# Gating of expert blocks in two steps, and a denser order of the last state-space scan, in a Perceiver layer

## The chip, the cores and the metric

The kernel runs on one core of a Trainium2 chip. The metric is the device time of one execution in microseconds (us). A profile is one execution taken by the hardware profiler; its times count from the start of its span.

## What is computed

`x` is 4 batches of 256 tokens of width 256, `ctx` 4 batches of 4096 context rows. Three residual layers follow each other, each on a layernorm of `x`:

```
x = x + xattn(layernorm(x), ctx)     # 8 heads of 64; keys and values from ctx and from x itself
x = x + mixed(layernorm(x))          # router: the top 64 tokens of a batch -> attention, the other 192 -> state-space model
x = x + moe(layernorm(x))            # 8 experts of hidden width 512, the best 2 of each token

# state-space core of `mixed` (per batch, 192 tokens, 512 channels, 16 states)
xi, z = split(u @ in_w); xc = silu(conv4(xi)); delta = softplus(dtp @ dt_w + dt_b)
h_t = exp(delta * A) * h_{t-1} + delta * xc * B_t;   y_t = sum over states of C_t * h_t
y = (y + xc * Dp) * silu(z) @ out_w

# one expert
y = (silu(x @ w_gate.T) * (x @ w_up.T)) @ w_down.T
```

The router ranks the 256 scores of a batch (how many are greater, ties by index), and a permutation built from the ranks puts the chosen tokens behind the others.

## The kernel before, in words

All is float32. The cross attention fills the first 1270 us or so: 16 groups (a batch and a pair of heads), each in 8 steps, with the order of every engine's work written out by hand. Beside it run "generators" for the other two layers: pieces of work that end in `yield due, cost`. A clock in the program (`now`) is moved on by hand-given lengths of the main work; at each call of `slot(budget)` (line 1168) every generator that is due and whose VectorE cost fits into what is left of the budget gets one step. So the numbers behind `yield` decide where on each engine's queue a piece stands. Each engine then works its queue in order and waits on semaphores.

Once the cross attention is done, batch 3 has still to go through `mixed` while the routed experts of the first six token tiles (batches 0 to 2) are at work. This is the stretch that the change touches:

- `ordered` (line 1687) works through 19 blocks of 128 gathered tokens. Block j has a gate half (`half(j, 0)`, tile p0b, 16 matmul passes) and an up half (p1b) into PSUM tiles of one tag with three buffers, then `turn_block(j + 1)` (transposes of the next block's rows into psxb, on TensorE, then a copy xTb on ScalarE), then the down half of block j - 1 (pdb, line 1746, from its gated tile hb), then the gating of block j. Weights are loaded three blocks ahead through SP's queue, rows gathered through GpSimd's.
- `gated` (line 1675) is tanh on ScalarE (line 1678), (tanh + 1) * gate on VectorE (line 1679, tile sg, which frees the gate half's PSUM buffer) and the product with the up half on VectorE (line 1683, tile hb, which frees the up half's).
- `router` (line 232) for batch 3: layernorm on ScalarE, transposes psxn, hidden psh, scores pssc, then the ranks on VectorE in two halves of 128 tokens (lines 288 to 296), `top` (line 300), positions psn, permutation `perm`, gathered tokens psg.
- `ssm_front`/`front_late` (line 603): four psin products with a convolution on VectorE each, then pspr, then psdt and the softplus (Abs, Exp, Ln on ScalarE, lines 669 to 675), then eight small products.
- `ssm_scan_late` (line 777): 16 steps (4 state groups by 4 channel tiles). A step is four exponentials on ScalarE (`decay`, one step ahead, three buffers), and on VectorE a product (line 838), the scan itself (839), a product (845) and an addition (846) into a tile `db` of a tag with four buffers; `sums` (line 810) then adds it into PSUM with two matmuls by the identity, one step behind. B and C come by broadcasting loads on ScalarE's queue (line 795), two state groups ahead.
- `ssm_back` (line 857): gate, out_w product (pssd), back to token order (psback), residual; then `prepare` (line 1810): layernorm, transposes (psx, line 1824), router logits (pslg) for the dense experts. `experts` (line 1852) runs all 8 experts on batch 3's two tiles, pg and pu (line 1868) and pde (line 1881); it needs `prepare`.

Of the kernel before, what the change touches and what calls it, by code (L numbers as in the profile page):

```python
# [8 lines left out]
F32 = mybir.dt.float32  # L9
AF = mybir.ActivationFunctionType  # L10
ALU = mybir.AluOpType
# [3 lines left out]
P = 128  # L15
# [9 lines left out]
NBOT = T - KTOP  # L25
DIN, DS, DC, DTR = 512, 16, 4, 16
NDT = DIN // P
# [19 lines left out]
def perceiver_layer(ctx: ExitStack, tc: tile.TileContext, a: dict, out: bass.AP):  # L47
    nc = tc.nc
# [183 lines left out]
    def router(b, st):  # L232
# [21 lines left out]
        for c in range(KD):  # L254
# [7 lines left out]
            out=lower, in_=lower, compare_op=ALU.is_gt, fill=0.0, base=0,  # L262
# [3 lines left out]
        hs = bg.tile([P, 2, T], F32, tag="r3", name="hT_srow")  # L266
# [21 lines left out]
        for h in range(2):  # L288
            eq = bg.tile([P, T], F32, tag="r4", name="eq")
            for other, op0, op1 in (  # L290
                (lower[:, h, :], ALU.is_equal, ALU.mult), (eq, ALU.is_gt, ALU.add),
            ):
                nc.vector.scalar_tensor_tensor(
                    out=eq, in0=srow, scalar=scol[:, h : h + 1], in1=other, op0=op0, op1=op1
                )
            nc.vector.tensor_reduce(out=rank[:, h : h + 1], in_=eq, axis=AX.X, op=ALU.add)
            if h == 0 and not late:
                yield 0.5, 1.6
        top = small.tile([P, 2], F32, name="top")
        nc.vector.tensor_scalar(  # L300
            out=top, in0=rank, scalar1=float(KTOP), scalar2=None, op0=ALU.is_lt
        )
        yield (4.5 if late else 1.0), 1.4

        ps = bank("psn")
        nc.tensor.matmul(ps[:, 0:1], cs["tri"], top[:, 0:1], start=True, stop=True)
# [296 lines left out]
    def front_late(b, st, ws, conv):  # L603

        ua, xc, zs, delta = st["ua"], st["xc"], st["zs"], st["delta"]
        pool = late["pool"]
        th = pool.tile([P, NDT, NBOT], F32, tag="ul", name="th")
        pss = {}  # L610

        def silu(m):
            nc.vector.scalar_tensor_tensor(
                out=xc[:, m, :], in0=th[:, m, :], scalar=1.0, in1=xc[:, m, :],
                op0=ALU.add, op1=ALU.mult,
            )

        st["dt_w"] = pool.tile([DTR, DIN], F32, name="dt_wl")
        nc.scalar.dma_start(out=st["dt_w"], in_=a["dt_w"])
        yield 0.9, 0  # L620
        for m in range(NDT + 2):
            if m < NDT:
                ps = pss[m] = bank("psin")
                for j in range(2):
                    for c in range(KD):
                        nc.tensor.matmul(
                            ps[:, j * NBOT : (j + 1) * NBOT], ws[m][:, j, c, :],
                            ua[:, c, :NBOT], start=(c == 0), stop=(c == KD - 1),
                        )
                nc.scalar.activation(  # L630
                    xc[:, m, :], ps[:, :NBOT], AF.Identity, bias=cs["conv_b"][:, m : m + 1],
                    scale=cs["conv_w"][:, m, DC - 1 :],
                )
                nc.scalar.activation(zs[:, m, :], ps[:, NBOT : 2 * NBOT], AF.Copy, scale=0.5)
            if 1 <= m <= NDT:
                conv(m - 1, pss[m - 1])
                nc.scalar.activation(th[:, m - 1, :], xc[:, m - 1, :], AF.Tanh)
            if m >= 2:
                silu(m - 2)
            yield 0.9, 0  # L640
        projT = bg.tile([DTR + 2 * DS, NBOT], F32, tag="projT", name="projT")
        ps = bank("pspr")
        for m in range(NDT):
            nc.tensor.matmul(
                ps[: DTR + 2 * DS, :NBOT], cs["xproj"][:, m, :], xc[:, m, :],
                start=(m == 0), stop=(m == NDT - 1),
            )
        nc.scalar.copy(projT, ps[: DTR + 2 * DS, :NBOT])

        bcd = st["bcd"] = dram.tile([2, DS, NBOT], F32, tag="bcd", name="bcd")  # L650
        nc.scalar.dma_start(
            out=bcd.rearrange("o s t -> (o s) t"), in_=projT[DTR:, :]
        )
        st["late"] = ssm_scan_late(b, st)
        yield 0.9, 0

        ev = bg.tile([P, NDT, NBOT], F32, tag="y", name="ev")
        for i in range(2):
            ps = bank("psdt")
            for j in range(2):  # L660
                m = 2 * i + j
                nc.tensor.matmul(
                    ps[:, j * NBOT : (j + 1) * NBOT], st["dt_w"][:, m * P : (m + 1) * P],
                    projT[:DTR, :], start=True, stop=True,
                )
            for j in range(2):
                m = 2 * i + j
                v = ps[:, j * NBOT : (j + 1) * NBOT]
                nc.scalar.activation(ev[:, m, :], v, AF.Abs, bias=cs["dt_b"][:, m : m + 1])
                nc.vector.tensor_scalar(  # L670
                    out=delta[:, m, :], in0=v, scalar1=cs["dt_b"][:, m : m + 1], scalar2=0.0,
                    op0=ALU.add, op1=ALU.max,
                )
        nc.scalar.activation(ev, ev, AF.Exp, scale=-1.0)
        nc.scalar.activation(ev, ev, AF.Ln, bias=1.0)
        next(st["late"])
        yield 5.4, 0
        u = st["u"] = pool.tile([P, NDT, NBOT], F32, tag="ul", name="ul")
        for m in range(NDT):
            nc.vector.tensor_tensor(delta[:, m, :], delta[:, m, :], ev[:, m, :], ALU.add)  # L680
            nc.vector.tensor_tensor(u[:, m, :], xc[:, m, :], delta[:, m, :], ALU.mult)
            if m == 0:
                next(st["late"])
        st["scanning"] = True
# [92 lines left out]
    def ssm_scan_late(b, st):  # L777
# [3 lines left out]
        SG = 4  # L781
        K = DS // SG
# [27 lines left out]
        def sums(i):  # L810
            k, m = divmod(i, NDT)
            for s in range(SG // 2):
                nc.tensor.matmul(
                    yps[:, m // 2, (m % 2) * NBOT : (m % 2 + 1) * NBOT], ident, dbl[i][:, s, :],
                    start=False, stop=(k == K - 1 and m % 2 == 1 and s == SG // 2 - 1),
                )

        dbl = {}
# [1 line left out]
        load(1)  # L820

        yps = st["yps"] = late["psum"].tile([P, 2, 512], F32, name="yps")
        zero = pool.tile([P, SG, NBOT], F32, tag="dbl", name="zero", bufs=4)[:, :2]
        nc.gpsimd.memset(zero, 0.0)
        for i in range(2):
            nc.tensor.matmul(
# [7 lines left out]
        for i in range(K * NDT):  # L834
            k, m = divmod(i, NDT)
            decay(i + 1)
            db = dbl[i] = pool.tile([P, SG, NBOT], F32, tag="dbl", name="db", bufs=4)
            nc.vector.tensor_tensor(db, spread[k, 0], bc(u[:, m, :], 1, SG), ALU.mult)
            nc.vector.tensor_tensor_scan(
                out=db.rearrange("p s t -> p (s t)"),  # L840
                data0=das[i % 3].rearrange("p s t -> p (s t)"),
                data1=db.rearrange("p s t -> p (s t)"),
                initial=0.0, op0=ALU.mult, op1=ALU.add,
            )
            nc.vector.tensor_tensor(db, db, spread[k, 1], ALU.mult)
            nc.vector.tensor_tensor(db[:, : SG // 2], db[:, : SG // 2], db[:, SG // 2 :], ALU.add)
            if i:
                sums(i - 1)
            if m == NDT - 1:
                load(k + 2)  # L850
            if i == 5:
                start(gate_late(b, st))
            yield 3.9, 3.8
        sums(K * NDT - 1)
        yield 1.5, 0

# [791 lines left out]
    with ExitStack() as s4, tc.manual_schedule():  # L1648
# [23 lines left out]
        def load_expert(e):  # L1672
            return [load_part(e, i) for i in range(3)]

        def gated(pg, pu, out, n):

            sg = fk.tile([P, 512], F32, name="sg")
            nc.scalar.activation(sg[:, :n], pg[:, :n], AF.Tanh, scale=0.5)
            nc.vector.scalar_tensor_tensor(
                out=sg[:, :n], in0=sg[:, :n], scalar=1.0, in1=pg[:, :n],  # L1680
                op0=ALU.add, op1=ALU.mult,
            )
            nc.vector.tensor_tensor(out, sg[:, :n], pu[:, :n], ALU.mult)

        first = {}

        def ordered():
# [72 lines left out]
            for j in range(4):  # L1760
                gather(j)
            turn_block(0)
            for j in range(NB):
                pg = yield from half(j, 0)
                load(j + 3, 0)
                pu = yield from half(j, 1)
                load(j + 3, 1)
                turn_block(j + 1)
                gather(j + 4)
                rest = down(j - 1)  # L1770
                yield next(rest, 0.9)

                hs[j] = fk.tile([P, NHC, P], F32, name="hb")
                gated(pg, pu, hs[j].rearrange("p m i -> p (m i)"), 512)
                yield from rest
                if j:
                    load(j + 2, 2)
# [115 lines left out]
        while "ready" not in order:  # L1893
            now[0] += 1.0
            slot(5.0)
        late["prepare"] = prepare
        now[0] += 1.0
        slot(5.0)
        for took in ordered():
            now[0] += took  # L1900
            slot(5.0)
        while "x4T" not in dense:
# [50 lines left out]
```

## Time and profile before

| | us |
|---|---|
| median of the runs (lowest, highest) | 1538.34 (1537.46, 1538.44) |
| the profiled execution's own time | 1534.16 |
| its span | 1532.4 |
| busy: TensorE matmul, VectorE, ScalarE, GpSimd | 1452.4, 1062.5, 758.1, 411.9 |
| end of the last cross attention matmuls (po, line 1449) | 1272.3 |
| first scan step of batch 3 (line 838) | 1327.5 |
| end of the last scan step (line 846) | 1422.2 |
| first dense expert matmul (pg, line 1868) | 1441.9 |

A row of the trace gives the start, the length, the engine, the line, the operation, the tiles written and read, their sizes and how many instructions are merged into it; in square brackets stands the idle time of the engine before it and what ended that. The granted clock is the share of TensorE's full clock that it was allowed. A float32 matmul shows as two passes, so one psum group of 4 by 2 matmuls is a row of 16. Ends of matmuls are modelled, and rows that follow each other overlap a little.

### The profile page before, as it was taken

To read this page: it belongs to the slowest core of one execution; us is meant where nothing else is said; L and a number is where in the kernel's file an instruction comes from. 1 tells how busy PE (TensorE), PEld (TensorE's weight loads), DVE (VectorE), ACT (ScalarE), POOL (GpSimd) and SP (SyncE) were. 2 spreads that over 40 slices of the span, in tenths; PEclk is the share of its full clock that TensorE was granted. 3 is DMA by queue.
4 is the path that set the end of the run, shared out by engine and by line. 5 is a ranking of instruction groups with operands and counts; after the bars stand their busy time and mean duration, and the time that the engine had idled before them with its cause. 6 is when DMAs were issued, how large, how long until landed. Compare 5 with 4: busy or idle time off the path is not lost.

```text
span 1532.4 us, 37303 instructions
## 1 busy us (share of the span) xinstructions
PE 1452.4 (95%) x15686; PEld 1034.5 (68%) x15686; DVE 1062.5 (69%) x1825; ACT 758.1 (49%) x1484; POOL 411.9 (27%) x465
## 2 busy tenths in 40 slices
PE   7999999999999999999999999999998968899899
PEld 3657676677666566675756665757574757888687
DVE  1666665656589986565899956666999663689453
ACT  3444454455566645454766544656655523544211
POOL 1000000000069960000499800001999101210110
PEclk9999999999999999999999999999999979999999
DMA  6455434424345443424445444352643333788461
GB/s 229 142 158 152 157 116 150 154 85 131 109 145 179 138 131 121 148 82 144 144 135 174 135 134 130 103 163 73 182 157 99 105 131 109 244 272 283 136 203 49
DMA packets 157767, 223.41 MB, mean 146 GB/s; under 512 B 14976, under 2 KB 76160, under 8 KB 157600
## 3 DMA queue, kind: packets, MB, share of 16 engines
q1 hardware_dynamic: 149632, 208.96, 43.3%
q10 hardware_dynamic: 6480, 8.00, 1.6%
q0 software_dynamic: 1488, 4.07, 1.0%
q8 instruction: 124, 2.03, 0.5%
q14 instruction: 43, 0.35, 0.1%
HBM read 216.56 MB, written 4.42 MB: 144 GB/s over the span
## 4 chain that ended last, share of the span: by engine, by line
PE 65%; POOL 15%; DVE 11%; issue 4%; ACT 2%; DMA 1%; SPq 0%; ACTq 0%; DVEq 0%; POOLq 0%
PE po L1449 12%; PE su L1383 11%; PE psv L1367 11%; PE psk L1330 9%; POOL y L751 6%; POOL db L736 5%; POOL db L749 5%; DVE sp L1403 3%; PE su L1391 2%; PE pg L1868 2%; PE pu L1868 2%; PE pde L1881 2%; PE p1b L1732 2%; DVE db L743 1%; DVE pt L1440 1%
## 5 line engine op out<-in xcount | busy, mean ns | idle before, releaser
L1403 DVE TENSOR_SCALAR_CACHE_REDUCE sp<-su 128x1088 f32<-128x1088 f32 x256 | 318.8, 1282 | 181.9 <-PE su L1391 181.9
L1440 DVE STREAM_TRANSPOSE pt<-sp 128x1088 f32<-128x1088 f32 x256 | 328.0, 1295 | 57.4 <-PE po L1449 57.4
L1431 ACT ACTIVATE sp<-sp,nb 128x1088 f32<-128x1088 f32 x256 | 305.1, 1195 | 13.4 <-DVE nb L1420 13.2
L1449 PE MATMUL po<-pt,v 128*64 128x128 f32 x4352 | 261.9, 277 | 2.3 <-DVE pt L1440 1.3
L1383 PE MATMUL su<-kt,qz 64*32 64x512 f32 x4096 | 255.5, 607 | 4.4 <-DVE nb L1420 3.7
L1330 PE MATMUL psk<-ctx,wk 128*128 128x512 f32 x512 | 245.5, 612 | 10.5 <-DMA ctx<-in_ctxT 7.8
L1367 PE MATMUL psv<-wv,ctx 128*128 128x128 f32 x2048 | 250.3, 279 | 0.5 <-DMA ctx<-in_ctxT 0.3
L1449 PEld LDWEIGHTS po<-pt,v 128*64 128x64 f32 x4352 | 240.0, 138 | 13.9 <-issue 7.5
L1367 PEld LDWEIGHTS psv<-wv,ctx 128*128 128x128 f32 x2048 | 236.1, 192 | 6.6 <-issue 1.3
L1330 PEld LDWEIGHTS psk<-ctx,wk 128*128 128x128 f32 x512 | 91.4, 192 | 95.6 <-issue 86.0
L1318 ACT COPY kt<-psk 128x512 f32<-128x512 f32 x128 | 74.9, 585 | 157.7 <-PE psk L1330 157.5
L1383 PEld LDWEIGHTS su<-kt,qz 64*32 64x32 f32 x4096 | 63.3, 107 | 123.6 <-issue 94.3
L751 POOL TENSOR_TENSOR y<-y,db 128x192 f32<-128x192 f32 x192 | 135.5, 706 | 15.1
L1371 ACT COPY v<-psv 128x512 f32<-128x512 f32 x144 | 79.3, 558 | 119.4 <-PE psv L1367 118.0
L743 DVE TENSOR_TENSOR_SCAN db<-da,db 128x384 f32<-128x384 f32 x96 | 122.7, 1279 | 13.2 <-POOL db L736 2.5
L749 POOL TENSOR_TENSOR db<-db,cb 128x384 f32<-128x384 f32 x96 | 111.3, 1159 | 24.3 <-DVE da L741 24.3
L395 POOL TENSOR_TENSOR kbd<-qk,hmask 128x512 f32<-128x512 f32 x8 | 9.1, 1156 | 402.6 <-ACT qk L385 402.6
L736 POOL TENSOR_TENSOR db<-bb,xc 128x384 f32<-128x384 f32 x96 | 111.2, 1180 | 0.2
L1391 PEld LDWEIGHTS su<-kt,qz 128*32 128x32 f32 x2048 | 34.5, 109 | 108.9 <-issue 108.9
L731 ACT ACTIVATE da<-delta,A_log_sb 128x192 f32<-128x192 f32 x192 | 75.6, 447 | 52.7 <-DVE da L741 39.7
L1486 ACT COPY ao<-po 128x128 f32<-128x128 f32 x32 | 8.5, 264 | 149.8 <-PE po L1449 149.8
L1415 PEld LDWEIGHTS su<-mq,same 128*128 128x128 f32 x256 | 41.1, 192 | 54.8 <-DVE mq L1410 37.0
(298 smaller groups left out, 1582.1 us busy)
## 6 DMA issues: line engine op xcount, KB each, us to landing
ctx<-in_ctxT SPq DMA_DIRECT2D x256, 512.0 KB, 5.0
gateT<-in_gateT SPq DMA_DIRECT2D x27, 512.0 KB, 4.6
upT<-in_upT SPq DMA_DIRECT2D x27, 512.0 KB, 4.7
downT<-in_downT SPq DMA_DIRECT2D x27, 512.0 KB, 5.7
bb<-bcd SPq DMA_DIRECT2D x24, 192.0 KB, 3.8
cb<-bcd SPq DMA_DIRECT2D x24, 192.0 KB, 3.9
wv<-in_wv SPq DMA_DIRECT2D x32, 128.0 KB, 2.5
in_w<-in_in_w SPq DMA_DIRECT2D x32, 128.0 KB, 2.4
```

Of the source, the lines that this page charges most:

```text
L736: nc.gpsimd.tensor_tensor(db, bbs[k], bc(xc[:, m, :], 1, SG), ALU.mult)
L743: nc.vector.tensor_tensor_scan(out=db, data0=da, data1=db, initial=0.0, op0=ALU.mult, op1=ALU.add,)
L749: nc.gpsimd.tensor_tensor(db, db, cbs[k], ALU.mult)
L751: nc.gpsimd.tensor_tensor(y[:, m, :], y[:, m, :], db[:, s, :], ALU.add)
L1330: nc.tensor.matmul(ps, wqk[G][:, 0, c, :], ct[:, c, :], start=(c == 0), stop=(c == KD - 1),)
L1367: nc.tensor.matmul(ps[:, i * P : (i + 1) * P], lhsT, wv[G][:, w, c, :], start=(c == 0), stop=(c == KD - 1),)
L1371: nc.scalar.copy(v.rearrange("p k d -> p (k d)"), ps[:, : n * P])
L1383: nc.tensor.matmul(su[q * 32 : (q + 1) * 32, SC[j] + lo : SC[j] + lo + 512], qT[r, j, s * 32 : (s + 1) * 32], kt[r, q, lo : lo + 512], sta ...
L1403: nc.vector.tensor_scalar(out=sps[n][j], in0=su[:, SU[j] : SU[j] + QK], scalar1=1.0, scalar2=None, op0=ALU.mult, op1=ALU.max, accum_out=nm ...
L1431: nc.scalar.activation(sps[n][j], sps[n][j], AF.Exp, bias=nbs[n][:, j : j + 1], accum_out=lss[b][:, hp, s, j : j + 1],)
L1440: nc.vector.transpose(pts[m, j][:, i, :], sps[n][j])
L1449: nc.tensor.matmul(pos[m][j * HD : (j + 1) * HD, :], vts[m // 2, k // 4][:, k % 4, j * HD : (j + 1) * HD], pts[m, j][:, :, kk * 32 : (kk + ...
```

## The change

Six edits, all in the stretch after the cross attention:

- the gating of a block is split: tanh and the first VectorE step are issued in the middle of the block's up half, the product with the up half where the whole gating stood;
- batch 3's ranks get a `yield` between the two halves, as the other batches have, and a shorter one behind them;
- the wait between softplus and the first scan step is due after 3.6 instead of 5.4, a scan piece after 3.5 instead of 3.9;
- the sums of a step are issued two steps behind instead of one, and the tag `dbl` gets a fifth buffer;
- `ordered` yields once right after `turn_block(0)`, and this first step is taken ahead of the slot in which batch 3's router starts.

```diff
@@ router
-            if h == 0 and not late:
-                yield 0.5, 1.6
+            if h == 0:
+                yield (0.9 if late else 0.5), 1.6
...
-        yield (4.5 if late else 1.0), 1.4
+        yield (2.7 if late else 1.0), 1.4
@@ front_late
         next(st["late"])
-        yield 5.4, 0
+        yield 3.6, 0
@@ ssm_scan_late
-        zero = pool.tile([P, SG, NBOT], F32, tag="dbl", name="zero", bufs=4)[:, :2]
+        zero = pool.tile([P, SG, NBOT], F32, tag="dbl", name="zero", bufs=5)[:, :2]
...
-            db = dbl[i] = pool.tile([P, SG, NBOT], F32, tag="dbl", name="db", bufs=4)
+            db = dbl[i] = pool.tile([P, SG, NBOT], F32, tag="dbl", name="db", bufs=5)
...
-            if i:
-                sums(i - 1)
+            if i > 1:
+                sums(i - 2)
...
-            yield 3.9, 3.8
+            yield 3.5, 3.8
+        sums(K * NDT - 2)
         sums(K * NDT - 1)
@@ the expert stage
-        def gated(pg, pu, out, n):
+        def silu(pg, n):
             sg = fk.tile([P, 512], F32, name="sg")
             nc.scalar.activation(sg[:, :n], pg[:, :n], AF.Tanh, scale=0.5)
...
-            nc.vector.tensor_tensor(out, sg[:, :n], pu[:, :n], ALU.mult)
+            return sg
+
+        def gated(pg, pu, out, n):
+            nc.vector.tensor_tensor(out, silu(pg, n)[:, :n], pu[:, :n], ALU.mult)
...
             turn_block(0)
+            yield 0.0
             for j in range(NB):
                 pg = yield from half(j, 0)
                 load(j + 3, 0)
-                pu = yield from half(j, 1)
+                up = half(j, 1)
+                yield next(up)
+                sg = silu(pg, 512)
+                try:
+                    while True:
+                        yield next(up)
+                except StopIteration as end:
+                    pu = end.value
                 load(j + 3, 1)
                 turn_block(j + 1)
                 gather(j + 4)
                 rest = down(j - 1)
                 yield next(rest, 0.9)
                 hs[j] = fk.tile([P, NHC, P], F32, name="hb")
-                gated(pg, pu, hs[j].rearrange("p m i -> p (m i)"), 512)
+                nc.vector.tensor_tensor(
+                    hs[j].rearrange("p m i -> p (m i)"), sg, pu, ALU.mult
+                )
...
         late["prepare"] = prepare
+        blocks = ordered()
+        next(blocks)
         now[0] += 1.0
         slot(5.0)
-        for took in ordered():
+        for took in blocks:
```

## The prediction

> **What bounds the kernel now.** I read the page first (is TensorE the bound over all?), then the busy time by stretch (where it is not), then the rows of VectorE, ScalarE and TensorE around each idle stretch. On the page TensorE is the bound:
>
> ```profile
> PE 1452.4 (95%) x15686; PEld 1034.5 (68%) x15686; DVE 1062.5 (69%) x1825; ACT 758.1 (49%) x1484; POOL 411.9 (27%) x465
> ```
>
> The instruction order of the two programs is the same up to the first turn of a block's rows, at 1272.7 us, so only the stretches after that matter. Columns: stretch, length, busy time of PE, PEld, DVE, ACT and POOL, granted clock, DMA share, GB/s.
>
> ```profile
> 1272.40:1293.20 20.80, 15.02 (x96) 13.17 (x97) 8.68 (x21) 9.22 (x18) 2.85 (x3) 0.92 0.42 120
> 1293.20:1327.50 34.30, 33.84 (x234) 30.95 (x233) 15.38 (x39) 18.07 (x39) 4.10 (x8) 1.00 0.66 196
> 1327.50:1422.10 94.60, 86.89 (x624) 79.92 (x624) 87.32 (x96) 42.59 (x114) 11.59 (x11) 0.98 0.87 280
> 1422.10:1441.90 19.80, 14.22 (x79) 11.06 (x78) 6.78 (x15) 5.59 (x12) 1.55 (x2) 1.00 0.51 161
> 1441.90:1456.10 14.20, 13.26 (x56) 11.19 (x57) 7.68 (x26) 2.85 (x6) 4.87 (x6) 0.88 0.21 61
> ```
>
> They are: router of batch 3 beside the first blocks; front of its SSM; its scan; its end; dense expert 0. In the scan VectorE is busy as much as TensorE, and TensorE's figure is flattering, since its rows include waits inside groups: its matmuls there, counted by the steady length of each group, come to some 82 us. So the scan runs at VectorE's pace. Head and end are waits:
>
> ```profile
> 1286.30 0.17 DVE L300 TENSOR_SCALAR top<-rank 128x2 f32<-128x2 f32 x1
> 1286.38 0.69 DVE L1679 SCALAR_TENSOR_TENSOR sg<-sg,p0b 128x512 f32<-128x512 f32 x1
> ```
>
> ```profile
> 1281.59 2.00 PE L1732 MATMUL p0b<-xTb,gateT 128*128 128x128 f32 x16
> 1287.13 2.51 PE L1732 MATMUL p1b<-xTb,upT 128*128 128x128 f32 x16 [3.53 <-DVE sg L1679]
> ...
> 1440.15 0.33 PE L1824 MATMUL psx<-ident,x4l 128*128 128x128 f32 x1 [3.40 <-ACT x4l L211]
> ...
> 1441.87 1.83 PE L1868 MATMUL pg<-x4Tl,gateT 128*128 128x256 f32 x4 [0.68 <-ACT x4Tl L1828]
> ```
>
> The first gating stands behind the ranking on VectorE, so the second block's up half gets its PSUM buffer 3.5 us late; and after the scan nothing is left for TensorE but the chain through batch 3's last layernorm.
>
> **Head, part by part.** *Rows turned first* (`blocks = ordered(); next(blocks)`): on ScalarE the copy xTb of block 0 moves ahead of the layernorm's table load. The rows are turned at 1273.1 in both, so the copy can end at 1273.5 instead of 1275.62; the load (1.28) still ends at 1274.8, when the moments (1274.84) are ready, so the layernorm loses nothing. TensorE gains little: it then waits for the layernormed rows (1276.95) ahead of psxn. With x_sb scaled next to it, only 0.25 us reach pssc (1280.8 for 1281.06).
> *Gating in two steps, ranks in two*: VectorE now runs sg of block 0 at 1281.35, first half of the ranks (3.0 us, as in the trace), hb, second half (1.5): 1282.1 + 3.0 + 0.7 + 1.5, so `top` at 1287.4 rather than 1286.4. The 3.5 us wait goes, but psn now stands ahead of the next transposes and block 0's down half: TensorE is through p0b and p1b of block 1 at 1285.25 and waits 2.2 us for `top`. psn 0.6, psxb 0.2, pdb 1.7, half of p0b: psg at 1290.9 for 1295.09.
> *Then 1.55 us go*: pdb of block 1 has to take the PSUM buffer of the second psin, which its convolution frees at 1301.4 (sg of block 2 is now in between), where TensorE stands at 1299.87. psdt follows at 1309.45 (1313.43 before, with 1.95 us of psxb and pdb ahead of it that come later now).
> *A new wait*: psdt is now issued ahead of the transposes of block 4. Their copy xTb then queues on ScalarE behind the softplus, and with it block 4's first matmul and everything on TensorE:
>
> ```profile
> 1317.00 1.28 ACT L674 ACT_TABLE_LOAD   x1
> 1318.30 0.84 ACT L674 ACTIVATE ev<-ev 128x768 f32<-128x768 f32 x1
> 1319.16 1.28 ACT L675 ACT_TABLE_LOAD   x1
> ...
> 1320.45 0.84 ACT L675 ACTIVATE ev<-ev 128x768 f32<-128x768 f32 x1
> ...
> 1321.20 0.35 ACT L1726 COPY xTb<-psxb 128x256 f32<-128x256 f32 x1
> ```
>
> From psdt's start to the end of that row is 7.86 us (1313.43 to 1321.29); TensorE has psdt, yps, psxb, pdb, 4.85 us, to do. So it stops for some 3.4 us, until 1317.75. Scan: softplus done 1317.3, eight small products 2.7 us, so the first L838 at 1320.05 instead of 1327.54, 7.5 us earlier (bbl must land within 4.8 us of its issue; the weights' 512 KB take 4.6).
>
> **The scan.** One step and one block on VectorE:
>
> ```profile
> 1390.45 0.95 DVE L838 TENSOR_TENSOR db<-bbl,ul 128x768 f32<-128x768 f32 x1
> 1391.44 1.76 DVE L839 TENSOR_TENSOR_SCAN db<-dal,db 128x768 f32<-128x768 f32 x1
> 1393.23 0.96 DVE L845 TENSOR_TENSOR db<-db,cbl 128x768 f32<-128x768 f32 x1
> 1394.22 0.56 DVE L846 TENSOR_TENSOR db<-db 128x384 f32<-128x384 f32 x1
> 1394.70 0.68 DVE L1679 SCALAR_TENSOR_TENSOR sg<-sg,p0b 128x512 f32<-128x512 f32 x1
> 1395.48 0.69 DVE L1683 TENSOR_TENSOR hb<-sg,p1b 128x512 f32<-128x512 f32 x1
> 1396.09 0.95 DVE L838 TENSOR_TENSOR db<-bbl,ul 128x768 f32<-128x768 f32 x1
> ```
>
> A step takes 4.27 us (4.24 to 4.43 in the other rows), a gating 1.39. Before: 16 x 4.27 = 68.3, 12 gatings 16.7, the attention's and gate's products 3.9, 1.3 where kbd on GpSimd slows two products, idle 3.9: 94.1, the trace has 94.6. After: pieces at 3.5 instead of 3.9 put 10 gatings inside, and sg, issued in the middle of the up half, finds its tanh done; two waits of 0.45 remain, where ScalarE holds the load of cbl until L845 of that step, and tanh and xTb behind it. So 68.3 + 13.9 + 3.9 + 1.3 + 1.2 = 88.6: the last step ends at 1408.65 (1422.1 before). Sums two pieces behind take TensorE's waits for L846 (3.37 once) away, but TensorE has some 13 us of slack here (77.3 us of matmuls in the 90.9 from 1317.75 to 1408.65), so they are worth nothing by themselves; the fifth buffer lets them be late. The two-step gating adds no instruction; SP's loads and GpSimd's gathers keep their order.
>
> **The end.** More blocks are left: sums 0.65, half p0b, p1b, psxb, pdb of block 15 (4.6), pssd 4.2, blocks 16 to 18 with psback, psx, pslg inside (3 x 3.58 + 2 x 0.22 + 4 x 1.73 + 1.74 + 0.45 + 0.8 = 21.1): 30.6 us without a wait, since batch 3's chain (psback to x4T, some 8 us) runs beside two blocks. The dense experts start at 1439.25 for 1441.87: 2.6 us. Expert 0 took 14.2 us before, later ones 10.37 (1466.47 to 1476.84); 0.8 of pslg now lies before it, its clock (0.88 in the row) and its wait for hTe go: 3.7 us. **Sum: 6.3 us** on the profiled execution's 1534.16. It lies 4.2 below the median of 1538.34, which differs from it by no stage that I can name; I take the difference over: **1532.0**.
>
> **A rule against it.** The Trainium skill, "TensorE: Matmul & The Clock Gate", section "Why this matters for your kernels", says to leave no gap over about 3 us between bursts of matmuls: a window of idleness halves the clock. The change makes two (3.4 at block 4; 3.2 at block 7, behind cbl). The trace agrees: after 3.53 us p1b took 2.51 (steady 1.95) and pdb 2.94 (1.89), 1.8 us in all; after 1.96 nothing. By the rule 2 x 1.8 = 3.6 go, and 2.7 are gained; by the rows both fall where TensorE has slack (13 us), so the price is 0. I take 0, and keep 3.6 for the range.
>
> **Rivals.** *VectorE keeps its waits*: idle 3.9 as before (2.7 more), and the first bbl lands as late as 6.5 us after issue (cbl's issue at 1320.57 released ScalarE at 1327.1), 1.7 more: gain 1.9, 1536.4. For it: DMA share 0.87 in the scan. Against: a later cbl, issued at 1377.94, was there at 1381.84.
> *TensorE becomes the scan's bound (slower)*: from block 5's pdb (1337.2) it has 59.4 us of matmuls in 71.5 us. If its many short stops in the scan hold the clock below 59.4/71.5 = 0.83 on average, the gating waits for matmuls. At 0.72: 82.5, so 11.0 more: 4.7 slower, 1543.0. Against: 0.98 granted there before.
> *It does not do what it says*: the scan starts no earlier. That loses 7.5 and makes it 1.2 slower; the order of instructions speaks against it.
>
> **Numbers.** A measurement of this kernel can tell about 0.2% (3.1 us) from no change. The sum 0.66 (1528 to 1535.2), VectorE's waits 0.21 (to 1540), slower 0.13. Range: below, another 4 us if head waits are smaller than worked out; above, into the second case.
>
> **What would show it.** L838 first near 1320; last L846 near 1409; ten gatings between; a wait near 3.4 at block 4's p0b by xTb, about 2 at psn; no row of 3.4 at L1824; expert 0 in 10.5. Wrong, if VectorE idles more than 3 us in the scan or the granted clock there falls below 0.85.

## The result, and the profile after

The changed kernel takes 1530.93 us (median of 6 runs, 1528.14 to 1532.81) against 1537.9 (6 runs, 1534.25 to 1540.35) for the kernel before beside it: ratio 0.9957, 95% interval 0.9939 to 0.9974. So it is faster, by 0.4% or 6.6 us (4 to 9.4 by the ends of the interval). Its profiled execution took 1528.17 us (span 1526.5), 5.99 less than the one of before. A second set of runs gave 0.996 (0.9946 to 0.9974).

The page's line of busy times shows the same numbers of instructions as before and no busy time more than 1% away from before's, so hardly any work was added or taken away:

```profile
PE 1452.0 (95%) x15686; PEld 1035.9 (68%) x15686; DVE 1060.2 (69%) x1825; ACT 758.0 (50%) x1484; POOL 415.3 (27%) x465
```

Busy time by stretch of the changed kernel, columns as in the prediction. The stretches: router, front, scan, end, dense expert 0.

```profile
1271.35:1291.15 19.80, 16.71 (x105) 14.21 (x105) 9.64 (x26) 9.22 (x18) 3.38 (x7) 0.91 0.43 127
1291.15:1320.91 29.76, 25.43 (x156) 22.61 (x155) 12.71 (x33) 16.32 (x34) 1.90 (x2) 0.96 0.57 171
1320.91:1408.92 88.01, 80.21 (x571) 73.66 (x569) 83.65 (x92) 40.89 (x110) 17.11 (x12) 0.98 0.84 262
1408.92:1439.80 30.88, 30.36 (x206) 27.59 (x207) 12.86 (x34) 10.26 (x20) 0.00 (x0) 1.00 0.70 218
1439.80:1450.17 10.37, 10.37 (x50) 9.13 (x49) 3.86 (x9) 1.90 (x5) 3.78 (x4) 1.00 0.71 231
```

The scan is 6.6 us shorter, the end 11 us longer and now full of TensorE's work (30.36 of 30.88 us), expert 0 at its steady length. VectorE's rows of the head show that block 0's first gating step stands ahead of the ranks, and that hb cuts the ranks in two:

```profile
1280.12 0.69 DVE L1680 SCALAR_TENSOR_TENSOR sg<-sg,p0b 128x512 f32<-128x512 f32 x1 [5.30 <-ACT sg L1679]
...
1283.28 0.42 DVE L296 TENSOR_REDUCE rank<-eq 128x1 f32<-128x256 f32 x1
1283.61 0.68 DVE L1787 TENSOR_TENSOR hb<-sg,p1b 128x512 f32<-128x512 f32 x1
...
1285.70 0.17 DVE L300 TENSOR_SCALAR top<-rank 128x2 f32<-128x2 f32 x1
1285.77 0.68 DVE L1680 SCALAR_TENSOR_TENSOR sg<-sg,p0b 128x512 f32<-128x512 f32 x1
```

TensorE's rows answer to the three waits shown of before. The 3.53 us at p1b and the 3.40 at psx are gone; there is one of 1.68 at psn, one of 3.18 at block 4's p0b and one of 2.99 at block 7's:

```profile
1282.29 1.95 PE L1736 MATMUL p1b<-xTb,upT 128*128 128x128 f32 x16
1285.92 0.38 PE L306 MATMUL psn<-top,tri 128*128 128x1 f32 x2 [1.68 <-DVE top L300]
...
1286.86 2.96 PE L1750 MATMUL pdb<-downT,hb 128*128 128x256 f32 x8
1289.62 1.70 PE L1736 MATMUL p0b<-xTb,gateT 128*128 128x128 f32 x8
...
1318.00 3.58 PE L1736 MATMUL p0b<-xTb,gateT 128*128 128x128 f32 x16 [3.18 <-ACT xTb L1730]
...
1342.59 2.08 PE L1736 MATMUL p0b<-xTb,gateT 128*128 128x128 f32 x8 [2.99 <-ACT xTb L1730]
...
1430.58 0.60 PE L1839 MATMUL psx<-ident,x4l 128*128 128x128 f32 x4
...
1439.80 1.03 PE L1883 MATMUL pg<-x4Tl,gateT 128*128 128x256 f32 x4
```

The wait at block 4 is the foreseen one: on ScalarE its copy stands right behind the last step of the softplus.

```profile
1316.84 0.84 ACT L675 ACTIVATE ev<-ev 128x768 f32<-128x768 f32 x1
...
1317.59 0.35 ACT L1730 COPY xTb<-psxb 128x256 f32<-128x256 f32 x1
```

VectorE has three kinds of waits left in the scan, 2.0 us in all (view of the waits, columns: us in total, times, longest); the one for bbl ends with the first step, so 1.5 us lie inside. Of the 6.6 us, two gatings fewer make 2.8 and the shorter waits (3.9 us before) make 2.4; the rest is in gaps too short for this view and in slightly shorter products:

```profile
DVE amx L425 <- PE psas L419: 0.8, 1, 0.8
DVE sg L1680 <- ACT sg L1679: 0.7, 2, 0.5
DVE db L838 <- DMA bbl<-bcd: 0.5, 1, 0.5
```

**Where the time came from.** The end of the attention moves by a few us between executions (1272.64 before, 1271.62 after, up to 1276.73 in the runs below), and no edit touches what lies ahead of it. So I take the tail of each profile: from the end of the attention's last copy `ao` to the end of the span. It is 259.8 us before and 254.9 after. In it TensorE idles 23.8 us before and 19.1 after; its busy time is 236.0 and 235.8. So in this pair of profiles the gain is TensorE's idle time, nothing else. By part (head to the first L838, scan, end to the first pg, the rest): 54.9, 94.7, 19.7, 90.5 before; 49.3, 88.0, 30.9, 86.7 after.

### The profile page after: what moved, and what is told of

Read it like the earlier page. It is cut to its first block, busy times and chain, and to the rows that moved or that the text cites. A ratio compares the mean times of both kernels' runs of the same rounds, so it can differ in the third digit from the quotient of the medians.

```text
span 1526.5 us, 37275 instructions
## 1 busy us (share of the span) xinstructions
PE 1452.0 (95%) x15686; PEld 1035.9 (68%) x15686; DVE 1060.2 (69%) x1825; ACT 758.0 (50%) x1484; POOL 415.3 (27%) x465
## 4 chain that ended last, share of the span: by engine, by line
PE 63%; POOL 15%; DVE 13%; issue 4%; ACT 2%; DMA 2%; SPq 0%; ACTq 0%; DVEq 0%; POOLq 0%
PE po L1450 12%; PE psv L1368 11%; PE su L1384 11%; PE psk L1331 9%; POOL y L751 6%; POOL db L736 5%; POOL db L749 5%; DVE sp L1404 3%; PE su L1392 2%; PE pde L1896 2%; PE pu L1883 2%; PE pg L1883 2%; DVE db L839 2%; DVE db L743 1%; DMA ctx<-in_ctxT 1%
## 5 line engine op out<-in xcount | busy, mean ns | idle before, releaser
L1432 ACT ACTIVATE sp<-sp,nb 128x1088 f32<-128x1088 f32 x256 | 305.2, 1195 | 13.3 <-DVE nb L1421 13.1
L1368 PE MATMUL psv<-wv,ctx 128*128 128x128 f32 x2048 | 250.2, 279 | 0.7 <-DMA ctx<-in_ctxT 0.5
```

Of the source, the lines that this page charges most:

```text
L1368: nc.tensor.matmul(ps[:, i * P : (i + 1) * P], lhsT, wv[G][:, w, c, :], start=(c == 0), stop=(c == KD - 1),)
L1432: nc.scalar.activation(sps[n][j], sps[n][j], AF.Exp, bias=nbs[n][:, j : j + 1], accum_out=lss[b][:, hp, s, j : j + 1],)
```

## Experiments

Theory V, the prediction's: the scan is VectorE's work and TensorE has 13 us to spare in it, so a wait of TensorE there costs nothing and the gain is the earlier scan with fewer gatings. Rival T: TensorE's waits and clock are what counts. Each ratio is to the kernel before in the same set of runs (e1 to e4, e5 to e8 and e9 to e12 are a set each). Tail, TensorE's idle time in the tail, and the tail's parts come from each run's profile:

| kernel | ratio (95%) | tail | idle | head, scan, end, rest |
|---|---|---|---|---|
| before | 1 | 259.8 | 23.8 | 54.9, 94.7, 19.7, 90.5 |
| changed | 0.9957 (0.9939, 0.9974) | 254.9 | 19.1 | 49.3, 88.0, 30.9, 86.7 |
| e8, changed again | 0.9960 (0.9946, 0.9974) | 254.8 | 18.9 | 49.1, 88.1, 30.9, 86.7 |
| e1, pieces 3.6 | 0.9942 (0.9920, 0.9965) | 250.2 | 15.3 | 47.6, 90.6, 21.5, 90.6 |
| e2, pieces 3.7 | 0.9945 (0.9928, 0.9961) | 253.5 | 17.8 | 47.6, 93.4, 21.6, 90.9 |
| e3, half the sums on TensorE | 0.9938 (0.9919, 0.9956) | 251.0 | 13.1 | 47.1, 85.7, 31.5, 86.7 |
| e4, turn first | 1.0009 (0.9996, 1.0022) | 265.0 | 24.6 | 53.2, 92.1, 33.0, 86.7 |
| e5, whole gating | 1.0000 (0.9989, 1.0011) | 262.1 | 24.5 | 49.7, 89.7, 36.1, 86.7 |
| e6, sums one behind | 0.9961 (0.9946, 0.9976) | 253.8 | 18.6 | 49.2, 87.1, 30.9, 86.7 |
| e7, pieces 3.55 | 0.9934 (0.9918, 0.9949) | 250.7 | 15.3 | 49.4, 88.5, 24.0, 88.8 |
| e9, split alone | 0.9970 (0.9959, 0.9981) | 257.0 | 19.9 | 54.8, 94.9, 16.9, 90.4 |
| e10, ranks whole | 1.0003 (0.9990, 1.0015) | 261.1 | 22.7 | 51.2, 88.6, 34.6, 86.7 |
| e11, 3.55 and half the sums | 0.9945 (0.9926, 0.9963) | 252.0 | 13.3 | 49.3, 85.9, 28.0, 88.8 |
| e12, copy on VectorE | 0.9987 (0.9976, 0.9998) | 257.6 | 22.9 | 49.7, 90.3, 30.9, 86.7 |

By the ratios alone, e4, e5, e10 and e12 are slower than the changed kernel; e1, e2, e3, e6, e9 and e11 are not told apart from it, since the intervals overlap. What is said of them below rests on one profile each, and in those of e1, e2 and e3 some 1.7 us of the tail are luck with the clock (last section).

**e1 and e2: the distance of the scan's pieces**, all else as in the changed kernel.

```diff
-            yield 3.5, 3.8
+            yield 3.6, 3.8
```

> The changed kernel with scan pieces at 3.6 instead of 3.5 in the planner's time; by the order of instructions 12 gatings then lie inside the scan (10 in the changed kernel) and two blocks fewer after it. Theory V (VectorE's chain sets the scan's length, TensorE has some 14 us to spare in it): the scan grows by 2 x 1.39 to 90.8 us, the stretch behind it shrinks from 30.9 to about 21.7 us (two blocks of 5.6 less, some 2 us more of work and waits at its end), expert 0 takes 0.8 more with the logits inside: 5.5 us faster than the changed kernel, some 1525.5 us, ratio to the kernel before 0.992; closer pieces are then a loss. Theory T (TensorE has no slack in the scan, or its clock takes it): the two blocks cost inside the scan what they cost behind it, and with the end's waits back it is 0 to 5 us slower than the changed kernel, ratio 0.996 to 0.999.

e2 has 3.7 there.

> The changed kernel with scan pieces at 3.7: 13 gatings inside the scan by the order of instructions, only two after it. Theory V: the scan 92.2 us, the stretch behind it about 20.5 us, expert 0 0.8 longer: 5.3 us faster than the changed kernel, ratio 0.992, with TensorE's slack nearly used up. Theory T: 1 to 6 us slower than the changed kernel, ratio 0.996 to 1.000.

In e1 scan (90.6) and end (21.5) came out as theory V has them; the ratio, 0.9942, did not reach V's 0.992. The closing layernorm is bare again, and expert 0 is back at before's pace, 3.9 us in place of the 0.8 expected. TensorE's rows of e1:

```profile
1433.20 0.33 PE L1839 MATMUL psx<-ident,x4l 128*128 128x128 f32 x1 [1.97 <-ACT x4l L211]
...
1434.91 2.00 PE L1883 MATMUL pg<-x4Tl,gateT 128*128 128x256 f32 x4 [0.67 <-ACT x4Tl L1843]
```

pg takes 2.00 for 1.03. From the scan's start on e1 gains 3.0 us on the changed kernel (202.6 for 205.6), not 5.5; the rest of its shorter tail is 1.7 us of clock in the head (last section). In its profile e2 fills the scan further and gives everything back: 205.9 for 205.6, where V expected 5.3 us less; its ratio is that of e1. So no gain by closer pieces (3.5) themselves is shown: they leave TensorE idle in the scan, and the ends differ by what covers the layernorm.

**e3: take work from VectorE, give it to TensorE.**

```diff
-            for s in range(SG // 2):
+            n = SG if i % 2 else SG // 2
+            for s in range(n):
...
-            nc.vector.tensor_tensor(db[:, : SG // 2], db[:, : SG // 2], db[:, SG // 2 :], ALU.add)
+            if not (i % 2):
+                nc.vector.tensor_tensor(
+                    db[:, : SG // 2], db[:, : SG // 2], db[:, SG // 2 :], ALU.add
+                )
```

> The changed kernel, but in every second scan step VectorE does not add the halves (L846) and TensorE sums four parts with the identity instead of two: 8 x 0.53 us less on VectorE, 8 x 0.65 us more on TensorE, the same result. Theory V: the scan is 4.3 us shorter (83.7), the rest as it was: 1526.6 us, ratio 0.993. Theory T: TensorE has 5.2 us more to do: 1536, ratio 0.999.

More work on TensorE, and the ratio is 0.9938, with T's 0.999 outside the interval: that speaks for V and against T. The scan is 2.3 us shorter, not 4.3, since VectorE then waits 3.0 us for the tanh (0.7 in the changed kernel).

**e4: take away the wait at block 4.** psdt is due after 1.8 instead of 0.9.

```diff
         st["late"] = ssm_scan_late(b, st)
-        yield 0.9, 0
+        yield 1.8, 0
```

> The changed kernel, but the matmuls psdt stand one piece later, behind the turn of block 4's rows and block 2's down half, so that the copy of block 4's rows no longer queues behind the softplus on ScalarE: the wait of 3.18 us at its first matmul and the 1.6 us of slow matmuls after it go; the scan starts about 2 us later. Theory V (a wait of TensorE ahead of the scan is covered by its slack): 1 to 2 us slower than the changed kernel, ratio 0.997. Theory T (waits and lost clock on TensorE are what counts): 2.8 to 4.8 us faster, ratio 0.993.

Neither: the tail is 10 us longer. The wait did not go, it moved to block 5, and there the decays stand ahead of its copy too; and block 4, turned ahead of psdt now, has its gate half done early, so that its tanh stands behind the softplus and its sg ahead of the scan's products: VectorE waits 5.8 us for it there. e10 shows the same rows (below).

**e5: undo the split of the gating.**

```diff
-                up = half(j, 1)
-                yield next(up)
-                sg = silu(pg, 512)
...
+                pu = yield from half(j, 1)
...
-                nc.vector.tensor_tensor(
-                    hs[j].rearrange("p m i -> p (m i)"), sg, pu, ALU.mult
-                )
+                gated(pg, pu, hs[j].rearrange("p m i -> p (m i)"), 512)
```

> The changed kernel with the gating whole again, both steps behind the up half; all else kept. VectorE has the same work ahead of the ranks' end, so top is where it was; the first gate half's PSUM buffer comes free some 2 us later, a wait of 1.9 us at block 1's p1b that takes the place of the one at psn. Theory V (the gain is the earlier scan, and the scan is VectorE's work): within 1.5 us of the changed kernel. Theory T (freeing the buffer early is what counts for TensorE): 4 to 5 us slower than the changed kernel, ratio 0.999.

The whole gain is gone, some 6 us, though the scan starts as early (49.7) and has as few gatings. Theory V, which expected 1.5 us at most, falls here; T had expected 4 to 5. The longest of TensorE's waits in e5's scan, and the view of all of them (us in total, times, longest):

```profile
1339.82 2.08 PE L1736 MATMUL p1b<-xTb,upT 128*128 128x128 f32 x8 [5.07 <-DVE sg L1680]
```

```profile
PE p1b L1736 <- DVE sg L1680: 11.8, 5, 5.1
```

The next block's up half needs the PSUM buffer that sg frees, and a whole sg stands behind a scan step on VectorE: five such waits in the scan, 11.8 us. The scan's row by stretch shows what they do:

```profile
1323.24:1412.97 89.73, 77.85 (x530) 71.84 (x529) 84.36 (x92) 38.36 (x105) 14.82 (x12) 0.92 0.74 238
```

TensorE gets through 530 instructions, against 571 in the changed kernel, at a clock of 0.92 instead of 0.98. What is missing is done after the scan: the end is 36.1 us for 30.9. So a wait of TensorE in the scan was not free here: it pushed work out of the scan.

This gives **theory R**: the tail is TensorE's work plus TensorE's idle time, and from the scan's end to the first pg the changed kernel has no idle time to give (0.5 us); an idle stop in the scan is free only as long as the work meant to be done in the scan still fits. The first half is true of any kernel, as an account; it is the last that can fail.

**e6: undo the sums two behind and the fifth buffer.**

```diff
...
-            db = dbl[i] = pool.tile([P, SG, NBOT], F32, tag="dbl", name="db", bufs=5)
+            db = dbl[i] = pool.tile([P, SG, NBOT], F32, tag="dbl", name="db", bufs=4)
...
-            if i > 1:
-                sums(i - 2)
+            if i:
+                sums(i - 1)
...
-        sums(K * NDT - 2)
```

> The changed kernel with the sums one piece behind and four buffers, as before; all else kept. Theory V: TensorE's wait for L846 (up to 3.4 us once) comes back inside its slack, no more than 0.5 us of difference. Theory T: 3 us slower, ratio 0.998.

No difference in the ratio, and the tail within 1.1 us of the changed kernel's (its scan is 1.0 shorter): this edit brings nothing here.

**e7: pieces at 3.55**, one block more in the scan instead of two.

> The changed kernel with scan pieces at 3.55: by the order of instructions 11 gatings inside the scan and one more sg, and batch 3's closing layernorm beside block 18's two halves and block 17's and 18's down halves. Theory V: scan 90.1 us, the stretch behind it 24.5 with no wait, expert 0 11.2: from the scan's start on 3.5 us less than the changed kernel (202.1 for 205.6), ratio 0.993 to 0.994, the best so far. Theory T: no faster than the changed kernel.

The lowest ratio of all: from the scan's start on 201.3 for 205.6. TensorE idles 2.3 us in its scan (7.8 in the changed kernel) and hardly waits after it, because blocks 17 and 18 lie around the layernorm:

```profile
1322.40:1410.90 88.50, 86.25 (x628) 80.47 (x627) 85.28 (x95) 42.83 (x114) 14.58 (x12) 0.98 0.87 286
```

```profile
1432.31 0.33 PE L1839 MATMUL psx<-ident,x4l 128*128 128x128 f32 x1 [0.73 <-ACT x4l L211]
...
1434.92 1.03 PE L1883 MATMUL pg<-x4Tl,gateT 128*128 128x256 f32 x4
```

Its 0.9934 lies below the changed kernel's 0.9960 from the same set. The intervals overlap a little, but each of its 6 runs (1525.11 to 1528.47 us) is faster than each of the changed kernel's 7 beside them (1528.70 to 1533.40). T, which expected no gain, fails here too.

**e8: the changed kernel again.**

> The changed kernel itself, on the chip and beside the runs of the kernels above: ratio 0.9957 as measured. If the slow rows behind the 1.68 us wait at psn are a matter of chance, this profile may lack them, and psdt then starts 36.5 us after the attention's end (38.2 in the first profile) as in the profiles with pieces at 3.6, 3.7 and with half the sums; if they belong to this program it starts at 38.2 again.

The slow rows behind psn are there again (psdt 38.2 us after the attention's end).

**e9: the split alone, on the kernel before.** The diff is the change's last hunk without the early first step.

> The kernel before with the gating in two steps and nothing else changed: TensorE's order is that of before, the scan starts after five gatings and has 12 inside. Refined theory R (two limits: the scan is VectorE's work, but TensorE comes out of it with a backlog as soon as its waits in the scan exceed some 14 us; the split takes the waits for p0b's buffer away): ahead of the scan the wait of 3.5 us and its 1.8 us of slow matmuls go, less a wait at the first down half for hb, in the scan 3.3 us of VectorE's waits for the tanh: 4 to 6 us faster than before, ratio 0.996 to 0.9975, the whole gain of the change or nearly. Theory W (the split only helps where the scan starts earlier and has fewer gatings inside): within 2 us of before.

0.3% or 4.6 us faster (2.9 to 6.3 by the ends of the interval): most of the gain. TensorE's waits for p1b are gone (3.5 us ahead of the scan and 3.2 in it before). R's size was right, one term was not: VectorE saves nothing in the scan, which is as long as before, since its waits there for the tanh are 2.9 us for 3.3, and 2.0 for 0.6 at amx. The profile shows only 2.8 us of the gain, all in the end. Its head is no shorter (54.8), but it had bad luck with the clock behind block 0's copy (last section): pssc starts 11.19 us after the attention's end, for 8.42 before, and psdt, at 40.9 for 40.8, has made up for that.

**e10: undo the two pieces of the ranks** (no `yield` between the halves, 4.5 behind `top`).

> The changed kernel with the ranks in one piece and 4.5 between top and the rank sums; all else kept. By the order of instructions the sums psn then stand behind block 1's turn and block 0's down half, and psdt behind the turn of block 4 as in the run with the turn first. Theory R: ScalarE's order is then that of that run: block 3's tanh waits behind the softplus, block 5's copy behind the decays, and it loses as that run did: 5 to 7 us slower than the changed kernel, ratio 0.999 to 1.001. Theory W (that run lost by chance or by its later psdt alone): within 2 us of the changed kernel.

As R expected, the gain is gone. (The tanh in question is block 4's; the expectation miscounts it as block 3's.) VectorE, ScalarE and TensorE of e10, one fence each:

```profile
1323.68 0.69 DVE L1680 SCALAR_TENSOR_TENSOR sg<-sg,p0b 128x512 f32<-128x512 f32 x1 [5.80 <-ACT sg L1679]
```

```profile
1323.06 0.60 ACT L1679 ACTIVATE sg<-p0b 128x512 f32<-128x512 f32 x1
...
1325.38 2.16 ACT L805 ACTIVATE dal<-delta,A_log_sb 128x191 f32<-128x191 f32 x6
1327.45 0.35 ACT L1730 COPY xTb<-psxb 128x256 f32<-128x256 f32 x1
```

```profile
1327.85 3.78 PE L1736 MATMUL p0b<-xTb,gateT 128*128 128x128 f32 x16 [5.41 <-ACT xTb L1730]
```

The order on ScalarE is softplus, tanh of block 4, decays, copy of block 5, the same as in e4, which lost about as much; the two share no edit. So I take the ranks to matter not for their own sake: their shorter piece puts psn ahead of a turn, and with it psdt ahead of block 4's turn, so that block 4's tanh and sg come behind the first scan step and hold up nothing.

**e11: e7 and e3 together.**

> Pieces at 3.55 and in every second step the halves summed on TensorE: the two that were faster than the changed kernel together. Theory R: VectorE 8 x 0.53 us less, of which waits for the tanh give half back as they did with pieces at 3.5, TensorE 8 x 0.65 us more in the 8 us that are left of its slack: 1 to 2 us faster than pieces at 3.55 alone, ratio 0.992 to 0.993. If the slack is used up already: 1 to 4 us slower than pieces at 3.55 alone.

Not the 1 to 2 us faster than e7 that R expected, but its other case: the scan is 2.6 us shorter than e7's, the end 4.0 longer, from the scan's start on 1.4 us more. (The ratios, from two sets, do not tell the two apart.) The row by stretch says why: TensorE is busy 85.87 of 85.91 us, and the bound has changed hands.

```profile
1321.58:1407.49 85.91, 85.87 (x631) 80.71 (x630) 80.68 (x87) 41.94 (x112) 14.29 (x12) 1.00 0.89 287
```

**e12: block 4's copy on VectorE.**

```diff
+                    if j == 4:
+                        nc.vector.tensor_copy(
+                            xTs[j].rearrange("p c i -> p (c i)"), ps[:, : KD * P]
+                        )
+                    else:
-                    nc.scalar.copy(xTs[j].rearrange("p c i -> p (c i)"), ps[:, : KD * P])
+                        nc.scalar.copy(xTs[j].rearrange("p c i -> p (c i)"), ps[:, : KD * P])
```

> The changed kernel, but the copy of block 4's turned rows is made by VectorE (which idles 3.3 us there for the softplus) instead of ScalarE, so that it does not stand behind the softplus. The wait of 3.18 us at block 4's first matmul goes. Theory R: TensorE can run ahead only as far as three PSUM buffers and ScalarE's next copy let it; it waits some 3 us at block 5 instead, the scan starts 0 to 0.3 us later: within 1 us of the changed kernel. Theory T (waits and lost clock on TensorE are what counts): 4 us faster, ratio 0.993.

The wait moved to block 5, as R has it, but grew: TensorE, ahead now, turns block 5's rows early and finds ScalarE at the decays.

```profile
1331.80 3.79 PE L1741 MATMUL p0b<-xTb,gateT 128*128 128x128 f32 x16 [7.42 <-ACT xTb L1735]
```

The ratio is 0.9987 for 0.996: R, which expected 1 us at most, missed this size, and T is wrong in its sign. A wait removed at one block is not a wait removed as long as the same queue serves the next.

## Why the prediction was right, and where it was not

- *Head.* The order came out as worked out: wait at psn 1.68 (2.2), at pdb of block 1 1.15 (1.55), at block 4's p0b 3.18 (3.4). `top` came 0.7 us sooner than forecast, measured from the attention's end. The scan starts 5.6 us earlier, measured from the attention's end, not 7.5. The step that failed is the price of the wait at psn: the prediction charged nothing for it, and pdb (2.96 for 1.89) and p0b (1.70 for 1.06) ran slow, 1.7 us in all. In e1, e2 and e3, with the same order up to there but without slow rows, the scan starts 7.3 to 7.8 earlier.
- *Scan.* 88.6 forecast, 88.0 measured, with ten gatings. That VectorE sets its length held for this kernel; TensorE's slack, 13 us by the prediction's count of steady lengths, shows as 7.8 us of idle time, and e11 shows where it ends.
- *End and expert 0.* 30.6 forecast, 30.88 measured; 10.5 and 10.37. pg starts 1.05 us earlier (from the attention's end), not 2.6: mainly the head's 1.7 us again. Expert 0 gains 3.9 (14.25 to 10.37; forecast 3.7). In sum 4.9 us, and another 1.0 of the pair's 6.0 is the attention's own earlier end, which no edit explains. So the total met 6.3 partly by luck.
- *The split "adds no instruction".* True, but the prediction gave it credit for the head alone. In the changed order it keeps TensorE from 11.8 us of waits for p0b's buffer in the scan; alone it gives 4.6 us (e9), without it nothing is left (e5). The earlier, shorter scan, which the prediction made its chief cause, moves one block from ahead of the scan and two from inside it to behind it; by itself it gained nothing (e5). So the size was right, and the mechanism only in part.
- *Closer pieces.* Counted with the right sign for the scan (6.6) and the end (11), but never set against the same change with other pieces. Slack of TensorE is work left undone: e7 puts one block into it and is about 4 us faster than the changed kernel (4.3 by the profiles, 3.6 by the medians).
- *Sums two behind, fifth buffer: worth nothing.* Confirmed by e6. *Rows first*: 0.25 us to pssc forecast, 0.38 measured (8.42 us after the attention's end before, 8.04 after); no run isolates it.
- *Price of the two new gaps, 0.* Not isolated: both attempts to take the wait at block 4 away (e4, e12) made a longer one. Both gaps did slow the matmuls behind them (p0b 3.58 for 1.95 at block 4, half of p0b 2.08 for 1.06 at block 7), as the rule has it; that this is free in the changed kernel is argued from the 7.8 us that TensorE idles in the scan anyway.
- *Rivals.* VectorE's waits inside the scan: 1.5 us in place of 3.9; the sum took 1.2. TensorE as the scan's bound: not here (0.98), but in e11, and in e5 by waits.

## What to carry to other kernels

Where one engine sets a stage's length, count what the other could have done in its slack: moving work into it until its idle time is nearly zero (e7) was worth more here than shortening the stage, and going on beyond that (e11) gave nothing more. In a ring of PSUM buffers, free each buffer by the earliest instruction that can, ahead of whatever long step shares that engine. And look at a wait to be removed through the queue that caused it: with everything in order behind one softplus, the next block's copy or tanh took the wait over here, and it grew (3.18 us to 5.4 in e4 and e10, to 7.42 in e12).

## What the hardware showed

Half clock after short waits, and not always: it goes by windows of 3.41 us. The wait for block 0's copy was 1.96 us in the kernel before and in e9; the 16 instructions behind it took 2.05 us in the one and 3.78 in the other:

```profile
1275.67 2.05 PE L1732 MATMUL p0b<-xTb,gateT 128*128 128x128 f32 x16 [1.96 <-ACT xTb L1726]
```

```profile
1274.22 3.78 PE L1735 MATMUL p0b<-xTb,gateT 128*128 128x128 f32 x16 [1.96 <-ACT xTb L1729]
```

Likewise the 1.68 us at psn cost 1.7 us in seven profiles with that order and nothing in three (e1 to e3). The traces show why. Their records of the granted clock, 1.00 or 0.50, change only at times that lie whole multiples of 3.413 us apart within a profile, in all fourteen. So the time can be cut into windows at these marks. Two neighbouring windows around psn of the changed kernel, then of e1, by the view by stretch (length, busy time of PE, PEld, DVE, ACT and POOL, clock, DMA share, GB/s):

```profile
1284.12:1287.53 3.41, 1.73 (x14) 1.53 (x13) 2.87 (x10) 0.37 (x1) 0.23 (x1) 1.00 0.82 250
1287.53:1290.95 3.42, 3.42 (x13) 2.97 (x12) 1.29 (x2) 0.37 (x1) 1.25 (x5) 0.50 0.22 77
```

```profile
1288.25:1291.66 3.41, 2.08 (x14) 1.95 (x15) 2.83 (x10) 0.37 (x1) 0.70 (x1) 1.00 0.69 235
1291.66:1295.07 3.41, 3.41 (x22) 3.08 (x21) 0.85 (x2) 0.37 (x1) 0.78 (x5) 1.00 0.49 122
```

In the changed kernel the whole wait falls into one window (1.73 us busy, 1.68 idle), and the next window runs at half clock, which costs half of 3.41 us: the 1.7 us. In e1 a mark cuts the wait, 1.33 us of it lie in the second window, and nothing follows. All seven slow profiles have 1.67 to 1.68 us idle in the window, the three others 1.31 to 1.34. It is the same with the copy, before and e9:

```profile
1271.49:1274.90 3.41, 1.85 (x20) 1.09 (x16) 1.32 (x4) 1.57 (x3) 0.95 (x1) 1.00 0.00 0
1274.90:1278.32 3.42, 2.65 (x23) 2.65 (x24) 0.42 (x3) 2.92 (x8) 0.00 (x0) 1.00 0.15 43
```

```profile
1270.21:1273.62 3.41, 1.68 (x17) 0.92 (x12) 1.32 (x4) 1.74 (x3) 0.95 (x1) 1.00 0.02 4
1273.62:1277.03 3.41, 2.81 (x13) 2.81 (x14) 0.42 (x3) 2.62 (x7) 0.00 (x0) 0.50 0.14 40
```

Over the tails of all fourteen profiles no full-clock window with up to 1.57 us idle was followed by one at half clock (943 windows), and of the 41 with 1.66 us or more 38 were; why three were not stays open.

The Trainium skill, "TensorE: Matmul & The Clock Gate", "Part 1: The HAM clock gate (the "warmup" mystery)", gives such a window, 3413 ns, and says that it runs freely and does not start anew with the kernel; the traces agree in length, and the marks lie differently against the program in each of them. That page has the clock fall after a window of idleness, and the rule that the prediction weighed allows gaps up to some 3 us; here about half a window was enough, so both are too mild for this case. Whether a wait of 1.7 to 2 us costs 0 or 1.7 us (or more, as in e9, where two windows in a row ran at half clock) is then a matter of where the marks fall, and the changed kernel drew the dear case in both of its profiles. For a sum it is to be priced between the two, not at 0 because one trace shows none.
